# Row 0's last tiles turned on another engine, fewer warming matmuls, and a new order of issue in a residual layer kernel

## The chip, the core and the metric

The kernel runs on one core of a Trainium2 chip, in one launch. The metric is the time of one execution on the device in microseconds, lower is better. TensorE (PE) multiplies matrices; VectorE (DVE), ScalarE (ACT) and GpSimd (POOL) work elementwise; SyncE (SP) issues nearly all DMAs, from one queue. Each of these engines takes its instructions strictly in the order in which they were issued, and waits on semaphores for what others make.

## The reference

```python
def _L0_cond_ref(hidden0, hidden1, x, W, b):
    hidden = jnp.concatenate([hidden0, hidden1], axis=-1)
    x_mean = jnp.mean(x, axis=1, keepdims=True)
    ...
    fused = jnp.concatenate([x, x_mean * ones_L, hidden[:, None, :] * ones_L], axis=-1)
    relation = jax.nn.relu(jnp.einsum('bld,do->blo', fused, W) + b)
    return relation
x = x + _L0_cond_ref(cond_512, cond_512, x, L0_cond_W, L0_cond_b)
```

x is 4 rows (batch) of 1024 positions of 512 numbers, W is 1536 by 512, all in 32-bit floats. The product splits into three: x times the first third of W, at every position; the mean of x over a row's positions times the second third, once a row; and the conditioning vector (used twice, 256 numbers) times the last third, once a row. The last two, with b, are one bias vector a row. The output is x plus the relu of product and bias.

## The kernel before, in words

**Tiles.** A tile is 128 positions of one row: 8 tiles a row, 32 in all. TensorE needs x with its 512 inputs on the partitions, in four chunks j of 128, so each tile is first turned (transposed), then multiplied. For accuracy x and W are each split in a high part that TensorE takes in its fast 32-bit format and the rest, a low part, and a chunk's product is three matmuls of 128x128 by 128x512: hi by w_hi, lo by w_hi, hi by w_lo (`product`, line 544). A tile takes 12 of them into one PSUM bank; 32 tiles take 384, of which the last tile's are cut in two column halves (24 matmuls of 256 columns and the same work).

**Two ways to turn.** A unit is 1 to 4 tiles of one row that are turned together, and a piece is what one split works on. Units listed in `BY_PE` are turned by TensorE: `turn` (line 428) issues one transpose of 128x128 per tile and chunk against an identity, from the x tile that is loaded as it lies. The others are turned by VectorE (line 441) from z, the same numbers loaded a second time in another arrangement, by four DMAs a unit (four quarters of 32 partitions in runs of 512 bytes); VectorE's transpose handles one chunk of a unit at a time. Row 0 is units 0 to 3 (tiles 0 to 3, one tile each, all four chunks in a piece) and unit 4 (tiles 4 to 7, a piece per chunk); all five are in `BY_PE`. The six units of rows 1 to 3 go by VectorE. Pieces are held in PSUM (two buffers, so a piece waits until the low part of the one two before it has been made) or, of VectorE's, every second in SBUF.

**What follows.** ScalarE writes hi (`split_hi`, line 446) and, for pieces of one chunk, adds up the positions in the same instruction; VectorE or GpSimd writes lo (`split_lo`, line 465). For the four whole-tile pieces VectorE adds up (`add_up`). When a row's pieces have been added up, VectorE reduces them to the total, ScalarE scales it and starts an accumulator with the conditioning part, VectorE runs four mean steps against w_mean (line 506), and upper, fold, rows_hi and rows_lo, on ScalarE and VectorE in turn, make two 64-partition operands; TensorE's bias product (`pb`, line 526) adds over the partitions and spreads the row's bias; ScalarE copies it. Then each accumulator is emptied: the first ten tiles (`PARK`) by a plain copy on ScalarE (line 570), since the bias is late, then bias, relu and x on GpSimd and ScalarE; others by VectorE with the bias; those in `BIAS_FIRST` start from a bias written ahead into the bank and need one VectorE instruction at the end. There are five accumulator banks, so a tile's first product waits until the tile five before it is emptied.

**Weights.** W's first third comes in four loads of 256 KB, each split in w_hi (ScalarE or VectorE, lines 419 and 421) and w_lo (VectorE or GpSimd, line 424). The first eight DMAs of SP are x tile 0, W 0, W 1, x 1, W 2, W 3, x 2, x 3.

**Warming.** `fill` (line 357) is a matmul of zeros into a bank that nothing reads. Five are issued at the start, and further ones wherever a model of the time, kept by the kernel, finds TensorE idle in its first 12 us (lines 602 to 604).

**What sets the order.** `make_plan` lists some 520 tasks with the engines that each may run on, a cost for each, and what it depends on. `ORDER` is a list of numbers: twice the task's number, plus one where the second of its engines is taken. The program is issued in that order, so it fixes every engine's sequence, SP's loads and stores among them, and the costs only place the warming matmuls. `PORTION` says in how many tiles' portions an x group of four is loaded (here: group 0 tile by tile, groups 5 to 7 in halves).

Of the kernel before, what the change touches and what calls it, by code (L numbers as in the profile page):

```python
# [23 lines left out]
G = 4  # L24
# [3 lines left out]
PORTION = {0: 1, 5: 2, 6: 2, 7: 2}  # L28
# [7 lines left out]
ROW0 = [(0, k, 1) for k in range(4)] + [(0, 4, G)]  # L36
# [61 lines left out]
SP = {"sp": (0.42, 0.42)}  # L98
ZQ = {"sp": (0.42, 0.42)}
MB = 2.62  # L100
# [24 lines left out]
def make_plan():  # L125
    plan = Plan()
    after = {}
    loads = [
        (("x", 0, 0), MB / 4), (("w", 0), MB / 4 + 1.6), (("w", 1), MB / 4 + 0.5), (("w", 2), MB / 4),
# [9 lines left out]
    first = list(chain.values())  # L139
    for s in range(2):  # L140
        plan.add(("w_cond", s), SP, [], pipe=MB / 2, soft=[("w_cond", 0)] if s else first)
    plan.add(("w_mean",), SP, [], pipe=MB + 0.5, soft=first)
# [16 lines left out]
    for n, g in enumerate(x_slots):  # L159
# [8 lines left out]
        for i in range(0, G, portion(g)):  # L168
            plan.add(("x", g, i), SP, deps, pipe=MB * portion(g) / G,
                     soft=chain + ([("w_cond", 1)] if n > x_slots.index("cond") else []))  # L170
# [6 lines left out]
    for c, (u, js) in enumerate(PIECES):  # L177
        r, k0, n = UNITS[u]
        whole = len(js) > 1
        w = n * len(js)  # L180
# [132 lines left out]
def kernel(  # L313
# [286 lines left out]
    for s, e, key in log:  # L600
        if e == "pe":
            if s < WARM_TO and s - pe_free > 0.35:
                for _ in range(int((s - pe_free - 0.1) / 0.22)):
                    fill()
            pe_free = s + plan.tasks[key][0][e][0]
        emit[key[0]](e, *key[1:])
# [28 lines left out]
```

## Time and profile before

| | us |
|---|---|
| runs, median (lowest, highest) | 107.23 (106.7, 107.62) |
| the profiled execution, its time | 106.93 |
| its span from first to last instruction | 105.1 |
| TensorE busy in it | 100.9 |
| VectorE busy | 73.7 |
| GpSimd busy | 71.2 |
| ScalarE busy | 61.3 |

The profile is one execution. A row of the timeline reads: start, how long, engine, line, operation, output from input, shapes, count; in square brackets the idle time just ahead and what ended it. A row of a stretch reads: from:to, length, and then for each engine in turn (PE, PEld, DVE, ACT, POOL) its busy time and number of instructions, last the granted clock, the DMA engines' share and their rate. A row of a group has busy time and mean nanoseconds of one behind the first bar, idle time ahead of it behind the second. PE's matmuls overlap (one of 512 columns is shown as 0.40 us long), so the distance of two starts tells more than a length. PEld is the load of the stationary operand, which overlaps PE.

### The profile page before, as it was taken

The page shows a single profiled execution, that of the slowest core. Times are in us where ns is not written, and L with a number is a line of the kernel's source. Part 1 is how long each engine was busy: PE and PEld are TensorE (multiplying, and loading weights), DVE is VectorE, ACT ScalarE, POOL GpSimd, SP SyncE. Part 2 cuts the span into 40 slices and gives each one's busy share as a digit, 9 for nine tenths or more (in the row PEclk, how much of TensorE's full clock was granted, in tenths as well). Part 3 has the DMA queues.
Part 4 walks back from the last instruction along what each step waited for, and adds up shares of the span by engine and source line. Part 5 has one row for each costly group of instructions (what it writes and reads, how often), then busy time and mean ns, then how long its engine had stood idle before and what let it go on. Part 6 is the DMA issues. An engine that isn't in the chain of part 4 may idle for free.

```text
span 105.1 us, 1449 instructions
## 1 busy us (share of the span) xinstructions
PE 100.9 (96%) x448; PEld 79.6 (76%) x448; DVE 73.7 (70%) x107; ACT 61.3 (58%) x136; POOL 71.2 (68%) x64
## 2 busy tenths in 40 slices
PE   5999999999999999999999999999999999999980
PEld 2447887888788878887888788788878887888870
DVE  1086575276999968999999999999989704500450
ACT  5244426899687997789995660999602206930000
POOL 6000407949748999999999999999999800791000
PEclk9999999999999999999999999999999999999999
DMA  3799999999999999999999999927989989755442
GB/s 65 224 305 379 388 417 252 171 200 197 201 176 235 169 202 203 204 204 225 356 390 388 215 199 274 368 108 235 342 262 375 403 280 306 280 212 199 157 161 81
DMA packets 23025, 26.31 MB, mean 250 GB/s; under 512 B 1253, under 2 KB 13801, under 8 KB 22890
## 3 DMA queue, kind: packets, MB, share of 16 engines
q1 hardware_dynamic: 23010, 26.22, 94.5%
q8 instruction: 3, 0.05, 0.2%
q14 instruction: 4, 0.03, 0.1%
q10 hardware_dynamic: 8, 0.00, 0.0%
HBM read 17.83 MB, written 8.39 MB: 249 GB/s over the span
## 4 chain that ended last, share of the span: by engine, by line
PE 96%; DVE 1%; issue 0%
PE po_None L554 83%; PE pw L358 5%; PE xT L439 4%; PE po L554 3%; PE pb L526 1%; DVE o L568 0%; DVE warm L346 0%; PE pt L475 0%; DVE one L348 0%
## 5 line engine op out<-in xcount | busy, mean ns | idle before, releaser
L554 PE MATMUL po_None<-w_hi,hi 128*128 128x512 f32 x124 | 48.8, 400 | 0.0
L554 PE MATMUL po_None<-w_hi,lo 128*128 128x512 f32 x124 | 48.7, 397 | 0.0
L554 PE MATMUL po_None<-w_lo,hi 128*128 128x512 f32 x124 | 48.4, 398 | 0.0
L581 POOL TENSOR_TENSOR o<-o,x 128x512 f32<-128x512 f32 x22 | 27.9, 1309 | 6.3 <-ACT o L578 6.3
L554 PEld LDWEIGHTS po_None<-w_hi,hi 128*128 128x128 f32 x124 | 23.3, 188 | 5.8 <-DVE w_hi L421 0.3
L554 PEld LDWEIGHTS po_None<-w_lo,hi 128*128 128x128 f32 x124 | 23.3, 188 | 5.5
L554 PEld LDWEIGHTS po_None<-w_hi,lo 128*128 128x128 f32 x124 | 23.3, 188 | 5.2
L441 DVE STREAM_TRANSPOSE xT<-z 128x512 f32<-128x512 f32 x24 | 25.1, 1090 | 1.0 <-DMA z<-in_x_dram 1.0
L452 ACT ACTIVATE hi<-xT 128x512 fp32r<-128x512 f32 x32 | 19.3, 608 | 8.6 <-PE xT L439 6.7
L468 POOL TENSOR_TENSOR lo<-xT,hi 128x512 fp32r<-128x512 f32 x12 | 15.5, 1313 | 2.4 <-ACT hi L452 2.3
L468 DVE TENSOR_TENSOR lo<-xT,hi 128x512 fp32r<-128x512 f32 x20 | 13.2, 678 | 4.1 <-ACT hi L452 4.0
L578 ACT ACTIVATE o<-o 128x512 f32<-128x512 f32 x22 | 13.4, 623 | 1.0 <-DVE o L572 0.6
L506 DVE SCALAR_TENSOR_TENSOR acc<-w_mean,tot,acc 128x512 f32<-128x512 f32 x16 | 12.1, 755 | 2.5 <-ACT acc L503 1.8
L575 POOL TENSOR_TENSOR o<-o,bias 128x512 f32<-128x512 f32 x10 | 12.9, 1312 | 0.1
L572 DVE TENSOR_TENSOR o<-po_None,bias 128x512 f32<-128x512 f32 x12 | 7.8, 675 | 5.0 <-issue 5.0
L568 DVE SCALAR_TENSOR_TENSOR o<-po_None,x 128x512 f32<-128x512 f32 x9 | 5.9, 682 | 7.1 <-PE po_None L554 5.6
L530 ACT ACTIVATE bias<-pb 128x512 f32<-128x512 f32 x4 | 2.4, 600 | 9.1 <-PE pb L526 9.1
L358 PE MATMUL pw<-warm 128*128 128x512 bf16 x14 | 5.8, 569 | 1.2 <-DVE one L348 1.2
L570 ACT ACTIVATE o<-po_None 128x512 f32<-128x512 f32 x10 | 5.6, 600 | 2.1 <-PE po_None L554 2.1
L424 POOL TENSOR_TENSOR w_lo<-w_x,w_hi 128x512 fp32r<-128x512 f32 x1 | 1.3, 1296 | 8.1 <-ACT w_hi L419 8.1
L461 DVE TENSOR_REDUCE sums<-xT 128x4 f32<-128x512 f32 x4 | 2.8, 689 | 5.1 <-ACT hi L452 5.1
L487 ACT ACTIVATE term<-wc,cT 128x512 f32<-128x512 f32 x8 | 5.5, 717 | 1.0 <-POOL wc L483 1.0
(45 smaller groups left out, 74.0 us busy)
## 6 DMA issues: line engine op xcount, KB each, us to landing
out_dram<-o SPq DMA_DIRECT2D x31, 256.0 KB, 5.7
z<-in_x_dram SPq DMA_DIRECT2D x24, 256.0 KB, 11.5
x<-in_x_dram SPq DMA_DIRECT2D x4, 1024.0 KB, 9.9
x<-in_x_dram SPq DMA_DIRECT2D x6, 512.0 KB, 7.2
x<-in_x_dram SPq DMA_DIRECT2D x4, 256.0 KB, 6.8
w_x<-in_L_cond_W_dram SPq DMA_DIRECT2D x4, 256.0 KB, 5.7
w_cond<-in_L_cond_W_dram SPq DMA_DIRECT2D x2, 512.0 KB, 8.2
w_mean<-in_L_cond_W_dram SPq DMA_DIRECT2D x1, 1024.0 KB, 12.2
```

The lines of the kernel that those rows point to most:

```text
L358: nc.tensor.matmul(pw, lhsT=warm[:, :P], rhs=warm, start=True, stop=True)
L441: nc.vector.transpose(v[:, : n * P].rearrange("p (n t) -> p n t", t=Q), zs[u].rearrange("p n (a j) -> p n j a", j=J)[:, : n * NQ, js[0], :],)
L452: nc.scalar.activation(hi[c][:, :m], xT[c][:, :m], AF.Copy, accum_out=sums[:, r, js[0], s : s + 1] if len(js) == 1 else None,)
L468: eng[e].tensor_tensor(lo[c][:, :m], xT[c][:, :m], hi[c][:, :m].bitcast(F32), ALU.subtract)
L506: nc.vector.scalar_tensor_tensor(acc[r], w_mean[:, j, :], totals[r][:, j : j + 1], acc[r], ALU.mult, ALU.add)
L554: nc.tensor.matmul(v[:, : m.shape[-1]], lhsT=(hi, lo, hi)[n][p][:, c * P : (c + 1) * P], rhs=m, start=(t not in BIAS_FIRST and i == 1), st ...
L568: nc.vector.scalar_tensor_tensor(o_tile(t)[:, d], v, 0.0, x_tile(t)[:, d], ALU.max, ALU.add)
L570: nc.scalar.activation(o_tile(t), v, AF.Copy)
L572: nc.vector.tensor_tensor(o_tile(t), v, biases[t // NK], ALU.add)
L575: nc.gpsimd.tensor_tensor(outs[t], outs[t], biases[t // NK], ALU.add)
L578: nc.scalar.activation(outs[t], outs[t], AF.Relu)
L581: nc.gpsimd.tensor_tensor(outs[t], outs[t], x_tile(t), ALU.add)
```

## The change

Tiles 4 to 7 were one unit turned by TensorE. They become two units of two tiles: tiles 4 and 5 are still turned by TensorE (`BY_PE` stays 0 to 4, and unit 4 is now the half), tiles 6 and 7 are unit 5, which is turned by VectorE from z. So eight transposes leave TensorE, four stream transposes of 256 columns come to VectorE, four z loads of 128 KB to SP, and x's second group is loaded in two halves, tiles 6 and 7 much later (they are needed at the end alone); the sixth group, before in two halves, is now loaded whole. Unit 4's pieces are half as wide, unit 5 adds four more: four hi and four lo of 512 columns become eight and eight of 256. The rule for warming matmuls asks for a longer gap and puts fewer in it. The order is a new list; the costs in the load table only shift the model.

```diff
-PORTION = {0: 1, 5: 2, 6: 2, 7: 2}
+PORTION = {0:1,1:2,6:2,7:2}
...
-ROW0 = [(0, k, 1) for k in range(4)] + [(0, 4, G)]
+ROW0 = [(0,k,1) for k in range(4)]+[(0,4,2),(0,6,2)]
...
-        (("x", 0, 0), MB / 4), (("w", 0), MB / 4 + 1.6), (("w", 1), MB / 4 + 0.5), (("w", 2), MB / 4),
+        (("x", 0, 0), MB / 4 + 0.25), (("w", 0), MB / 4 + 1.2), (("w", 1), MB / 4 + 1.0), (("w", 2), MB / 4 + 0.2),
...
-    plan.add(("w_mean",), SP, [], pipe=MB + 0.5, soft=first)
+    plan.add(("w_mean",), SP, [], pipe=MB + 0.8, soft=first)
...
-0 2 4 10 16 6 8 12 110 14 74 112 18 20 116 24 94 114 22 454 26 96 456 98 28 458 30 118 100 32 460 103 34 462 120
+0 2 4 10 16 6 8 12 118 14 120 18 103 122 486 105 488 124 82 20 490 106 24 108 492 111 113 26 28 126 128 494 496
...
             if s < WARM_TO and s - pe_free > 0.35:
-                for _ in range(int((s - pe_free - 0.1) / 0.22)):
+                for _ in range(int((s - pe_free - 0.35) / 0.43)):
                     fill()
```

The new list is one line longer, so behind it every line's number is higher by one: line 554 of the products is 555 there, 439 of the transposes 440. Three of the four w_lo are now GpSimd's (before, one), and three of the four w_hi VectorE's (before, one). In SP's order, behind the first eight loads, stood x's second group, the two w_cond, b, w_mean and row 1's z; now w_cond's first half, x's tiles 4 and 5, w_cond's second half, b, the four new z, w_mean, row 1's z.

The first place is TensorE at the head, from the last warming matmul behind tile 0's transposes to tile 1's transposes. pw is the warming matmuls' bank, po_None an accumulator, xT the turned x, a number behind a name its allocation. Before:

```order
L358 MATMUL pw<-warm 128x512
L554 MATMUL po_None<-w_hi,hi_134 128x512
L554 MATMUL po_None<-w_hi,lo_135 128x512
L358 LDWEIGHTS warm
L358 MATMUL pw<-warm 128x512
L554 MATMUL po_None<-w_lo,hi_134 128x512
L439 MATMUL xT_164<-ident,x_116 128x128 x4
```

And now:

```order
L359 MATMUL pw<-warm 128x512
L555 MATMUL po_None<-w_hi,hi_132 128x512
L555 MATMUL po_None<-w_hi,lo_133 128x512
L555 MATMUL po_None<-w_lo,hi_132 128x512
L555 MATMUL po_None<-w_hi,hi_132 128x512
L440 MATMUL xT_160<-ident,x_116 128x128 x4
```

The warming matmul between the second and the third product is gone, and a fourth product has moved ahead of the transposes; ahead of the piece, eight warming matmuls have become three.

The second place is VectorE around row 0's total (tot), its mean steps (acc from w_mean) and the first turns. Before:

```order
L468 TENSOR_TENSOR lo_257<-xT_245,hi_256 128x512
L468 TENSOR_TENSOR lo_290<-xT_275,hi_289 128x512
L496 TENSOR_REDUCE tot_306<-sums 128x4
L468 TENSOR_TENSOR lo_297<-xT_284,hi_296 128x512
L506 SCALAR_TENSOR_TENSOR acc_312<-w_mean,tot_306,acc_312 128x512 x4
L441 STREAM_TRANSPOSE xT_351<-z_155 128x512
L516 TENSOR_TENSOR acc_312<-acc_312,upper_353 64x512
```

And now:

```order
L442 STREAM_TRANSPOSE xT_293<-z_157 128x256
L442 STREAM_TRANSPOSE xT_295<-z_157 128x256
L442 STREAM_TRANSPOSE xT_306<-z_157 128x256
L469 TENSOR_TENSOR lo_304<-xT_295,hi_303 128x256
L497 TENSOR_REDUCE tot_312<-sums 128x4
L469 TENSOR_TENSOR lo_298<-xT_291,hi_297 128x256
L507 SCALAR_TENSOR_TENSOR acc_315<-w_mean,tot_312,acc_315 128x512 x4
L517 TENSOR_TENSOR acc_315<-acc_315,upper_360 64x512
L523 TENSOR_TENSOR rows<-acc_315,rows 64x512
L442 STREAM_TRANSPOSE xT_398<-z_240 128x512
```

The four turns of tiles 6 and 7 (the first is one row further up) now stand ahead of the total, and row 1's first turn (z_155 before, z_240 now) has moved behind fold and rows_lo.

The third place is ScalarE over the same time: the splits of the last pieces of row 0, the accumulator copies (o from po_None) and the conditioning's weighings (term). Before:

```order
L487 ACTIVATE term_1_282<-wc,cT 128x512
L452 ACTIVATE hi_289,sums<-xT_275 128x512
L452 ACTIVATE hi_296,sums<-xT_284 128x512
L570 ACTIVATE o_303<-po_None 128x512
L499 ACTIVATE tot_306<-tot_306 128x4
L503 ACTIVATE acc_312<-cond_280 128x512
```

And now:

```order
L453 ACTIVATE hi_297,sums<-xT_291 128x256
L453 ACTIVATE hi_300,sums<-xT_293 128x256
L453 ACTIVATE hi_303,sums<-xT_295 128x256
L453 ACTIVATE hi_308,sums<-xT_306 128x256
L504 ACTIVATE acc_315<-cond_287 128x512
L500 ACTIVATE tot_312<-tot_312 128x4
L488 ACTIVATE term_1_328<-wc,cT 128x512
L571 ACTIVATE o_330<-po_None 128x512
```

The second accumulator copy of the program (o_303 before, o_330 now, tile 1's) stood ahead of the total's scaling; now it stands behind the four hi of tiles 6 and 7, the accumulator's start, the scaling and a weighing.

37 rows, old and new, of the table ORDER are left out of this document.

## The prediction

> **What bounds the kernel now.** I read the page first, for shares and for the chain of waits.
>
> ```profile
> span 105.1 us, 1449 instructions
> PE 100.9 (96%) x448; PEld 79.6 (76%) x448; DVE 73.7 (70%) x107; ACT 61.3 (58%) x136; POOL 71.2 (68%) x64
> ...
> PE 96%; DVE 1%; issue 0%
> ```
>
> TensorE carries the chain. Whether it ever stands inside its 96% is for the chain in order of time and the busy time by stretches; I cut the stretches at the first product, at a product that waits, and where the waiting seems over.
>
> ```profile
> 7.08:9.43 2.35, 2.35 (x14) 1.61 (x12) 1.19 (x4) 0.92 (x2) 0.00 (x0) 1.00 1.04 344
> 9.43:12.26 2.83, 2.83 (x17) 2.52 (x17) 1.87 (x3) 1.10 (x3) 1.30 (x1) 1.00 1.05 395
> 12.26:101.97 89.71, 89.71 (x407) 72.96 (x405) 67.93 (x95) 56.26 (x129) 68.29 (x54) 1.00 0.99 252
> ```
>
> ```profile
> 65.49 21.71 PE po_None L554 x93
> ```
>
> 93 products in 21.71 us are 0.2334 us each, and from 12.26 on TensorE has no idle time: one instruction fewer there is its whole time saved. Busy time hides short waits, since a matmul of 0.40 us overlaps the next, so for the head I read TensorE's timeline by starts. (Row 0's products and the transposes are single rows; w_hi, w_lo are the split weights, hi, lo the split x.)
>
> ```profile
> 1.19 2.32 PE L358 MATMUL pw<-warm 128*128 128x512 bf16 x5 [1.19 <-DVE one L348]
> 3.47 1.10 PE L439 MATMUL xT<-ident,x 128*128 128x128 f32 x4
> 4.37 3.06 PE L358 MATMUL pw<-warm 128*128 128x512 bf16 x8
> 7.08 0.58 PE L554 MATMUL po_None<-w_hi,hi 128*128 128x512 f32 x1
> ...
> 9.14 0.39 PE L554 MATMUL po_None<-w_lo,hi 128*128 128x512 f32 x1
> 9.43 0.50 PE L554 MATMUL po_None<-w_hi,hi 128*128 128x512 f32 x1
> ...
> 11.87 0.64 PE L439 MATMUL xT<-ident,x 128*128 128x128 f32 x4
> 12.26 0.48 PE L554 MATMUL po_None<-w_hi,hi 128*128 128x512 f32 x1
> ...
> 18.63 1.12 PE L439 MATMUL xT<-ident,x 128*128 128x128 f32 x8
> 19.51 0.48 PE L554 MATMUL po_None<-w_lo,hi 128*128 128x512 f32 x1
> 19.82 0.40 PE L554 MATMUL po_None<-w_hi,lo 128*128 128x512 f32 x1
> ...
> 101.85 0.28 PE L554 MATMUL po<-w_lo,hi 128*128 128x256 f32 x1
> ```
>
> Two things: the warming matmuls stand before the first product and end just as it starts; and the seventh product, at 9.43, is the first one that a load decides. VectorE's timeline says which:
>
> ```profile
> 8.94 0.43 DVE L421 CAST w_hi<-w_x 128x512 fp32r<-128x512 f32 x1 [0.78 <-DMA w_x<-in_L_cond_W_dram]
> ```
>
> The third quarter of W lands at 8.94, its w_hi is made by 9.37, and TensorE goes on at 9.43.
>
> **The change part by part.**
>
> *Eight transposes fewer, the term that pays.* Tiles 4 to 7 cost TensorE 16 transposes, in two groups of 8. From 18.63 to 19.51 is 0.88; the product behind it takes 0.31 to the next start instead of 0.233, 0.08 more: 0.96 a group, 0.12 each. Now VectorE turns tiles 6 and 7, eight transposes go: **-0.97**, on the stretch without idle time.
>
> *Fewer warming matmuls, worth nothing in this execution.* By the orders on TensorE shown with the change, three warming matmuls stand behind the first transposes instead of eight, none between products, and a fourth product comes ahead of tile 1's transposes. What then decides each product:
>
> ```profile
> 4.61 0.60 ACT L452 ACTIVATE hi<-xT 128x512 fp32r<-128x512 f32 x1 [2.38 <-PE xT L439]
> 5.32 0.63 ACT L419 ACTIVATE w_hi<-w_x 128x512 fp32r<-128x512 f32 x1
> 6.81 0.63 ACT L419 ACTIVATE w_hi<-w_x 128x512 fp32r<-128x512 f32 x1 [0.86 <-DMA w_x<-in_L_cond_W_dram]
> ...
> 10.35 1.30 POOL L424 TENSOR_TENSOR w_lo<-w_x,w_hi 128x512 fp32r<-128x512 f32 x1 [8.08 <-ACT w_hi L419]
> ```
>
> The eight first loads keep their order. W's first quarter is there by 5.32; w_hi now comes by VectorE's cast (0.43): product 1 at 5.8, lo (0.68) product 2 at 6.4, w_lo by GpSimd (1.30) product 3 at 7.2, the second w_hi at 7.44 product 4 at 7.5, tile 1's transposes to 8.1, products 5 and 6 by 8.6. Product 7 waits for the same cast at 8.94: 9.43, as before. Behind it stand as many products and transposes as before up to 12.26 (14 and 16). So 1.3 us of earlier start ends in a wait of 0.9 us: **0**. GpSimd's other two w_lo, at 9.4 and 10.7, end by 12.0; TensorE asks for them at 13.0 and 14.4.
>
> The price in speed: five first warming matmuls in 2.32 us are (2.32 - 0.63) / 4 = 0.42 apart, double 0.2334 for as wide an operand. Eight in the 2.71 us from 4.37 to 7.08 fit 0.42 and then 0.22 with the turn near 6.5, though the granted-clock column reads 1.00 throughout. In the forecast this half speed costs nothing: even at 0.42, products 1 to 6 and four transposes end by 9.3, ahead of the load.
> [...]
>
> *What VectorE, ScalarE and the queue take on.* By VectorE's order, four half-width turns stand ahead of row 0's total and its mean chain, and the turns of row 1 now come behind that whole chain. Prices and landings:
>
> ```profile
> L441 DVE STREAM_TRANSPOSE xT<-z 128x512 f32<-128x512 f32 x24 | 25.1, 1090 | 1.0 <-DMA z<-in_x_dram 1.0
> L468 DVE TENSOR_TENSOR lo<-xT,hi 128x512 fp32r<-128x512 f32 x20 | 13.2, 678 | 4.1 <-ACT hi L452 4.0
> L506 DVE SCALAR_TENSOR_TENSOR acc<-w_mean,tot,acc 128x512 f32<-128x512 f32 x16 | 12.1, 755 | 2.5 <-ACT acc L503 1.8
> L542 ACT ACTIVATE po<-bias 128x256 f32<-128x256 f32 x2 | 0.7, 366 | 0.0
> ```
>
> ```profile
> 16.50 2.55 POOL L483 TENSOR_TENSOR wc<-w_cond 128x512 f32<-128x512 f32 x2 [4.86 <-DMA w_cond<-in_L_cond_W_dram]
> ```
>
> ```profile
> 20.42 0.69 DVE L468 TENSOR_TENSOR lo<-xT,hi 128x512 fp32r<-128x512 f32 x1 [2.27 <-ACT hi L452]
> ...
> 22.37 3.13 DVE L506 SCALAR_TENSOR_TENSOR acc<-w_mean,tot,acc 128x512 f32<-128x512 f32 x4 [0.56 <-ACT acc L503]
> 26.45 1.11 DVE L441 STREAM_TRANSPOSE xT<-z 128x512 f32<-128x512 f32 x1 [0.96 <-DMA z<-in_x_dram]
> ```
>
> ```profile
> L412 SPq DMA_DIRECT2D w_mean<-in_L_cond_W_dram x1: 357/357/357, 8.9 to 8.9; - x1
> ...
> DMA to landing us min/median/max: 12.2/12.2/12.2
> ```
>
> ```profile
> L386 SPq DMA_DIRECT2D x<-in_x_dram x1: 383/383/383, 5.3 to 5.3; - x1
> ...
> DMA to landing us min/median/max: 8.4/8.4/8.4
> ```
>
> A turn of 256 columns costs between 0.55 (half of 1.09) and 1.09; I take 0.55, since a copy of 128x256 takes 0.37 beside 0.60 whole. Four are 2.2 us, in a stretch where VectorE idled 2.27 and 0.96.
> When do the new z quarters land? w_mean landed at 8.9 + 12.2 = 21.1, row 1's four z by 26.45: 1.33 per 256 KB. w_cond landed at 16.5; x's second group, ahead of it, at 5.3 + 8.4 = 13.7, so w_cond's megabyte took 2.75. Half of that x no longer stands ahead, about 1.35 less: 15.1. Half a megabyte of z: 17.8. The upper bound: w_mean needed 4.6 where a megabyte takes 2.75, so a landing can lag 2: 19.8.
> At 17.8: turns to 20.0, the last hi near 21.4, total and scaling 22.1, four mean steps (3.13) 25.3, then upper, fold, rows_hi, rows_lo (0.6 to 0.7 each, on two engines, with other work of ScalarE's between) 28.5. TensorE comes to the bias product after 67 products from 12.26, the eight remaining transposes and the conditioning pair: 12.26 + 15.6 + 1.4 = 29.3. Spare: 0.8. Row 1's z land near 27.8 (1.33 later, for half a megabyte of z in place of half of x); VectorE turns from 28.4, the first lo is ready at 32.4 behind three turns, TensorE asks at 33.2. Spare: 0.8.
> ScalarE is tightest, since it is strictly in order. Tile 1's accumulator copy (o_330) stands behind the four new hi, the accumulator start, the scaling and a weighing; tile 6's first product needs that bank (the fifth after tile 1) at 12.26 + 46 products + 1.4 = 24.4. With z at 17.8 the copy ends near 23.4, spare 1.0; at 19.8 it ends near 24.5 and the bias product's inputs near 30, a wait of 0.1 to 0.7. I take **+0.1** (0 to 0.7), nearer the early bound, because in this place w_cond precedes z and not the late w_mean.
> The tail keeps its order: the last tile's two halves, one last store. **0.** Later rows keep their instructions; SP has four more issues, and z's bytes grow by 0.5 MB, in queues that TensorE never waited for.
>
> *Sum:* -0.97 + 0 + 0.1 = -0.87 against this execution's 106.93 (span 105.1 and 1.8 around it): 106.06. The runs' median is 107.23 (106.7 to 107.62), which would give 106.36. I centre on the middle of both, **106.2**.
>
> **The rivals.**
>
> *A. The new chain through ScalarE eats the gain.* Place: o_330 behind the z turns, and the bias product. If z lands beyond 19.8, every microsecond more is one on TensorE. For it: a spare of 1.0 against a lag of up to 2 that w_mean showed. Against: nothing lagged ahead of w_mean. Landing 0.7 beyond the bound: 106.2 + 0.7 = **106.9**.
>
> *B. The speed rises late, and the change is slower.* In the trace half speed ended 5.3 us after 1.19, without a break. If a break starts the count again, the changed kernel, whose unbroken activity ends at 5.65, counts from 9.43: half speed until 14.7, 5.3 / 0.42 = 12.6 products where 22.7 fit, 10.1 x 0.233 = 2.4 us lost: 106.2 + 2.4 = **108.6**. It erases the gain from the point where more than 0.87 / 0.19 = 4.6 products run slowly after 9.43, so if the rise is later than 11.4. Against: at half speed TensorE is busy nearly all of 5.8 to 9.3 anyway.
>
> *C. The third quarter of W lands earlier in most executions.* Then the earlier start is worth something: product 7 could follow at 8.6, 0.8 sooner, **105.4**. For it: landings of W took 4.1 to 6.5 us here:
>
> ```profile
> DMA to landing us min/median/max: 4.1/5.7/6.5
> ```
>
> Against: that order of loads is untouched, and one trace shows 8.94.
>
> **How the numbers follow.** Forecast 0.6, A 0.18, B 0.11, C 0.11. One per cent, 1.07 us, is about what a measurement tells here. The forecast's 106.2 is just under it from 107.23: of its 0.6, 0.29 fall over 1%. Faster 0.29 + 0.11 = 0.40; same 0.31 + 0.18 = 0.49; slower 0.11. The range, 105.4 to 107.3, takes in C, A, and the spread of the runs shown, and leaves B out.
>
> **What would show it.** Right: 24 transposes at 0.12 each, product 7 again at about 9.4 behind VectorE's cast, 12.26 unchanged, no idle TensorE behind it, the last product near 101.0 instead of 101.85, the bias product near 29.3. Wrong: a wait of tile 6's first product or the bias product (A), starts 0.42 apart behind 9.43 (B), product 7 before 9 (C), or a wait of row 1's first lo.

## The result: 0.6% faster, and the profile after

| | before | after |
|---|---|---|
| runs, median (lowest, highest), us | 107.06 (106.09, 108.76), 12 runs | 106.38 (105.52, 108.27), 12 runs |
| the profiled execution, its time | 106.93 | 106.00 |
| its span | 105.1 | 104.2 |
| TensorE busy in it | 100.9 | 99.3 |
| last product starts | 101.85 | 100.66 |

The ratio of the times is 0.9936, 95% interval [0.9908, 0.9965]: 0.68 us less, between 0.37 and 0.98. All ratios below are to the kernel before, run beside on the same chip, and leave out executions that took over 1.5% more than the fastest of the same kernel, which are 3 of the 12 of the changed kernel here and 0 to 9 of a kernel's executions below. The kernels were timed on several chips; the text says where two of them shared one.

The page of the changed kernel, in the lines that answer to those of before:

```profile
span 104.2 us, 1439 instructions
PE 99.3 (95%) x434; PEld 77.9 (75%) x434; DVE 75.3 (72%) x113; ACT 60.9 (58%) x142; POOL 75.0 (72%) x68
...
PE 90%; DMA 4%; POOL 1%; DVE 1%; SPq 0%; issue 0%
```

TensorE still carries the chain, with 14 instructions fewer (eight transposes and six warming matmuls), but 4% of the chain is now a load, W's, where the first products used to stand behind warming matmuls. The same three stretches, cut at product 1, product 7 and the first product behind tile 3's transposes (product 15):

```profile
6.17:9.12 2.95, 2.78 (x10) 1.76 (x11) 2.17 (x4) 0.90 (x2) 1.24 (x2) 1.00 1.00 382
9.12:11.92 2.80, 2.80 (x17) 2.42 (x17) 2.05 (x4) 0.93 (x2) 2.44 (x2) 1.00 1.05 394
11.92:100.78 88.86, 88.86 (x399) 71.98 (x397) 69.67 (x101) 56.99 (x136) 69.64 (x57) 1.00 1.01 261
```

The middle stretch is as long as before (2.80 against 2.83), the last one 0.85 shorter: it begins 0.34 earlier and the last product starts 1.19 earlier. TensorE's timeline of the changed kernel, by starts:

```profile
4.45 1.48 PE L359 MATMUL pw<-warm 128*128 128x512 bf16 x3
6.17 0.77 PE L555 MATMUL po_None<-w_hi,hi 128*128 128x512 f32 x1 [0.24 <-DVE w_hi L422]
...
8.89 0.40 PE L555 MATMUL po_None<-w_lo,hi 128*128 128x512 f32 x1
9.12 0.46 PE L555 MATMUL po_None<-w_hi,hi 128*128 128x512 f32 x1
...
13.41 0.39 PE L555 MATMUL po_None<-w_hi,hi 128*128 128x512 f32 x1
13.73 0.48 PE L440 MATMUL xT<-ident,x 128*128 128x128 f32 x2
...
28.90 0.40 PE L555 MATMUL po_None<-w_lo,hi 128*128 128x512 f32 x1
29.14 0.40 PE L527 MATMUL pb<-rows,ones 128*128 128x512 f32 x1
...
100.66 0.28 PE L555 MATMUL po<-w_lo,hi 128*128 128x256 f32 x1
```

Product 1 is 0.91 earlier and product 7 is 0.31 earlier. Tile 4's transposes start 0.32 behind the product ahead of them instead of 0.23: a wait of 0.09 for their x, which was not there before. The bias product (29.14) follows without a gap. VectorE's timeline shows what set the head and what the new chain cost:

```profile
5.60 0.43 DVE L422 CAST w_hi<-w_x 128x512 fp32r<-128x512 f32 x1 [4.32 <-DMA w_x<-in_L_cond_W_dram]
...
8.59 0.43 DVE L422 CAST w_hi<-w_x 128x512 fp32r<-128x512 f32 x1
...
19.29 2.21 DVE L442 STREAM_TRANSPOSE xT<-z 128x256 f32<-128x256 f32 x4
...
22.86 3.13 DVE L507 SCALAR_TENSOR_TENSOR acc<-w_mean,tot,acc 128x512 f32<-128x512 f32 x4 [0.27 <-DMA w_mean<-in_L_cond_W_dram]
```

The cast of W's third quarter starts at 8.59 (8.94 before), since the load landed earlier in this execution; product 7 follows it. The four turns are 0.55 us each. The mean steps wait for w_mean.

One part of the time lies behind the last transfer. These are SP's last events by the trace (start in us, the semaphores waited for), with the landing of the last store; no view of the page lists them:

```
before: 104.31 last store landed (semaphore 110)
        103.00 106 | 103.06 107, 105 | 103.12 108, 104 | 103.23 109, 101 | 104.33 110, 100 | 105.15 end
after:  103.13 last store landed (semaphore 106)
        103.14 106 | 103.20 107, 105 | 103.27 108, 104 | 103.33 109, 101 | 103.39 110, 100 | 104.22 end
```

In both traces SP checks the DMAs' semaphores at the end in the same order, some 0.065 us a step where none is waited for (the times are those at which a step was through). Before, the last store had the one that is checked last, and the other checks were over by then. The changed kernel has four transfers more (84 in its trace, 80 before), which moves the last store on to the one that is checked first, so four checks follow its landing: from landing to end it is 1.09 us instead of 0.84.

So the profiled pair's -0.93 is, to 0.01, -0.34 (head), -0.85 (behind product 15) and +0.25 (end).

### The profile page after: what moved, and what is told of

It reads as the page before. It is cut to its first block, busy times and chain, and to the rows that moved or that the text cites. A ratio compares the mean times of both kernels' runs of the same rounds, so it can differ in the third digit from the quotient of the medians.

```text
span 104.2 us, 1439 instructions
## 1 busy us (share of the span) xinstructions
PE 99.3 (95%) x434; PEld 77.9 (75%) x434; DVE 75.3 (72%) x113; ACT 60.9 (58%) x142; POOL 75.0 (72%) x68
## 4 chain that ended last, share of the span: by engine, by line
PE 90%; DMA 4%; POOL 1%; DVE 1%; SPq 0%; issue 0%
PE po_None L555 83%; DMA w_x<-in_L_cond_W_dram 4%; PE po L555 3%; PE xT L440 2%; POOL w_lo L425 1%; PE pb L527 1%; DVE w_hi L422 0%; DVE o L569 0%; SPq L387 0%; PE pt L476 0%
## 5 line engine op out<-in xcount | busy, mean ns | idle before, releaser
L555 PE MATMUL po_None<-w_hi,hi 128*128 128x512 f32 x124 | 49.4, 402 | 0.2 <-DVE w_hi L422 0.2
L555 PE MATMUL po_None<-w_hi,lo 128*128 128x512 f32 x124 | 49.3, 399 | 0.0
L442 DVE STREAM_TRANSPOSE xT<-z 128x512 f32<-128x512 f32 (+1 forms) x28 | 27.5, 1027 | 0.1
L453 ACT ACTIVATE hi<-xT 128x512 fp32r<-128x512 f32 (+1 forms) x36 | 20.0, 559 | 10.0 <-PE xT L440 7.1
L469 POOL TENSOR_TENSOR lo<-xT,hi 128x512 fp32r<-128x512 f32 (+1 forms) x14 | 17.0, 1218 | 0.8 <-ACT hi L453 0.8
L469 DVE TENSOR_TENSOR lo<-xT,hi 128x512 fp32r<-128x512 f32 (+1 forms) x22 | 13.1, 601 | 3.3 <-ACT hi L453 3.2
L425 POOL TENSOR_TENSOR w_lo<-w_x,w_hi 128x512 fp32r<-128x512 f32 x3 | 3.9, 1285 | 5.9 <-DVE w_hi L422 5.9
L513 ACT ACTIVATE upper<-acc 64x512 f32<-64x512 f32 x4 | 2.4, 598 | 7.3 <-DVE acc L507 7.2
L453 ACT ACTIVATION_READ_ACCUMULATOR hi<-xT 128x1 f32 x32 | 6.2, 192 | 0.0
```

The costliest lines, as they stand in the source:

```text
L442: nc.vector.transpose(v[:, : n * P].rearrange("p (n t) -> p n t", t=Q), zs[u].rearrange("p n (a j) -> p n j a", j=J)[:, : n * NQ, js[0], :],)
L453: nc.scalar.activation(hi[c][:, :m], xT[c][:, :m], AF.Copy, accum_out=sums[:, r, js[0], s : s + 1] if len(js) == 1 else None,)
L469: eng[e].tensor_tensor(lo[c][:, :m], xT[c][:, :m], hi[c][:, :m].bitcast(F32), ALU.subtract)
L555: nc.tensor.matmul(v[:, : m.shape[-1]], lhsT=(hi, lo, hi)[n][p][:, c * P : (c + 1) * P], rhs=m, start=(t not in BIAS_FIRST and i == 1), st ...
```

## The experiments

All but the second start from the changed kernel; the edit of each is shown.

**The old rule for warming matmuls.**

```diff
-                for _ in range(int((s - pe_free - 0.35) / 0.43)):
+                for _ in range(int((s - pe_free - 0.1) / 0.22)):
```

> The changed kernel with the old rule for warming matmuls (15 in all instead of 8; 7 instead of 3 behind tile 0's transposes, 3 more between the first products). Theory (the head waits for W's third quarter, the warming matmuls are cover): the first product moves from 6.2 to about 7.0, product 7 from 9.1 to between 9.1 and 9.5, since products 1 to 6 now end just after the load instead of before it; time +0.0 to +0.4 us on the changed kernel. Rival (the earlier start is what pays): the 0.9 us come back, ratio to the kernel before near 1.00.

Measured: 0.9934 [0.99, 0.9968]. TensorE's timeline of this kernel:

```profile
9.64 0.39 PE L555 MATMUL po_None<-w_hi,hi 128*128 128x512 f32 x1
...
12.41 0.48 PE L555 MATMUL po_None<-w_hi,hi 128*128 128x512 f32 x1
...
101.03 0.28 PE L555 MATMUL po<-w_lo,hi 128*128 128x256 f32 x1
```

Product 7 is 0.5 later than in the changed kernel's trace, though W's third quarter was cast earlier (by 8.83, there by 9.02): in this execution it stood behind the matmuls ahead of it and not behind the load. The ratio is the same, but it rests on seven of twelve executions, and the median of all twelve, 106.73, is only 0.2% under the 106.95 of the kernel before; the two rules are alike within some 0.4%. From product 15 to the last product it is 88.62, against 89.59 before: 0.97 less, with no wait in between.

**The new rule alone**, in the kernel before.

```diff
-                for _ in range(int((s - pe_free - 0.1) / 0.22)):
+                for _ in range(int((s - pe_free - 0.35) / 0.43)):
```

> The kernel before with only the new rule for warming matmuls (8 instead of 14). Theory: first product from 7.08 to about 6.0, product 7 stays at the landing of W's third quarter plus 0.5 us (near 9.4), all behind it as before; ratio to the kernel before 1.000 (0.998 to 1.002). Rival (earlier start pays): 0.991. Rival (half speed lasts longer without them): 1.01 to 1.02, with starts 0.42 apart behind 9.4.

Measured: 0.9984 [0.9951, 1.0017]. TensorE's timeline:

```profile
6.08 0.79 PE L554 MATMUL po_None<-w_hi,hi 128*128 128x512 f32 x1 [0.25 <-ACT w_hi L419]
...
9.00 0.39 PE L554 MATMUL po_None<-w_hi,hi 128*128 128x512 f32 x1
...
11.73 0.48 PE L554 MATMUL po_None<-w_hi,hi 128*128 128x512 f32 x1
...
101.30 0.28 PE L554 MATMUL po<-w_lo,hi 128*128 128x256 f32 x1
```

From 11.73 to 101.30 are 89.57, as before. The rule is worth nothing that these times can tell, with either order; the gain is the order's.

**Tiles 4 and 5 transposed twice on TensorE**, the second time into the same place: the eight transposes are back, and nothing else is.

```diff
-                    nc.tensor.transpose(v[:, (m * n + i) * P : (m * n + i + 1) * P], x_t[:, j], ident)
+                    for _ in range(2 if u == 4 else 1):
+                        nc.tensor.transpose(v[:, (m * n + i) * P : (m * n + i + 1) * P], x_t[:, j], ident)
```

> The changed kernel with the eight transposes of tiles 4 and 5 issued twice, into the same place, so that TensorE has 32 transposes again and nothing else changes. Theory: 8 x 0.12 = +0.97 us on the changed kernel, of which up to 0.1 may lie in TensorE's short wait for x's tiles 4 and 5; ratio to the kernel before near 1.002. Rival (the gain came from the order or the warming): the changed kernel's time, ratio near 0.994.

Measured: 1.0015 [0.9981, 1.0048], 0.79% above the changed kernel, some 0.85 us, which by the two intervals together is known to some 0.5 us. TensorE's timeline:

```profile
12.19 0.48 PE L556 MATMUL po_None<-w_hi,hi 128*128 128x512 f32 x1
...
13.68 0.39 PE L556 MATMUL po_None<-w_hi,hi 128*128 128x512 f32 x1
14.50 0.72 PE L441 MATMUL xT<-ident,x 128*128 128x128 f32 x4 [0.43 <-DVE sums L463]
...
102.42 0.28 PE L556 MATMUL po<-w_lo,hi 128*128 128x256 f32 x1
```

From 12.19 to 102.42 are 90.23, of which 0.59 is the wait ahead of tile 4's transposes (0.82 between starts less 0.23; by the trace's DMA events their x landed at 14.36, so the releaser named is not the one). The 89.64 left are 1.02 above the 88.62 of the kernel without waits. The eight transposes carry the gain.

**The last store back on the semaphore that is checked last**, by loading four x groups in halves (four transfers more, the same data).

```diff
-        nc.sync.dma_start(out=xs[g][:, i : i + n], in_=xv[r, :, k + i : k + i + n, :])
+        for a in range(i, i + n, 2 if n == G else n):
+            d = slice(a, a + (2 if n == G else n))
+            nc.sync.dma_start(out=xs[g][:, d], in_=xv[r, :, k + d.start : k + d.stop, :])
```

> The changed kernel with the four x groups that are loaded whole (2 to 5) loaded in two halves each, four DMAs more, so that the last store gets again the last of the eight semaphores that SP checks in turn at the end. Theory (the end costs 0.26 us more because the last store's semaphore is checked first and the others after it): last landing to the span's end falls from 1.05 to about 0.79 us, ratio to the kernel before near 0.991. Rival (the end's difference is chance, or a DMA's): stays at 1.05, ratio 0.994.

Measured: landing at 104.38, end at 105.21: 0.83 us between them, as the theory has it. The time does not settle more: the ratio of 0.9898 [0.984, 0.9957] rests on three of twelve executions (105.36, 105.63, 106.62), the others took 107.0 to 109.0.

**The changed kernel again**, for the spread.

> The changed kernel itself once more, beside the next three on one chip. Theory (transposes pay 0.85 to 0.97, the end gives 0.26 back): ratio to the kernel before 0.991 to 0.996, and a wider spread of its executions than of the kernel before's, since it waits for two landings (W's third quarter, x's tiles 4 and 5) where the kernel before waits for one. Rival (the spread of the first runs was chance): the same spread as the kernel before.

Measured: 0.9928 [0.989, 0.9966], median 106.24. The spread is wider, as expected: the twelve executions have a standard deviation of 0.7 us, the 35 of the kernel before beside them 0.5. Its trace, TensorE's timeline, has a wait that the first one had not:

```profile
28.93 0.40 PE L555 MATMUL po_None<-w_lo,hi 128*128 128x512 f32 x1
29.61 0.47 PE L527 MATMUL pb<-rows,ones 128*128 128x512 f32 x1 [0.28 <-DVE rows L523]
```

0.68 between starts is 0.45 of idle time ahead of the bias product.

**x of tiles 4 and 5 loaded ahead of w_cond** (82 is that load in the order's list, 18 is w_cond's first half).

```diff
-0 2 4 10 16 6 8 12 118 14 120 18 103 122 486 105 488 124 82 20 490 106
+0 2 4 10 16 6 8 12 118 14 120 82 18 103 122 486 105 488 124 20 490 106
```

> The changed kernel with the load of x's tiles 4 and 5 moved ahead of w_cond's first half in SP's order, nothing else. Theory (TensorE's wait ahead of tile 4's transposes is for this load, which the new order put 1.3 us later): the load lands near 12.3, the wait (0.1 in the first trace, 0.6 in another) is gone, w_cond as a whole lands as before; time -0.1 to -0.4 us on the changed kernel and a narrower spread. Rival (that wait is for the PSUM buffer, not the load): unchanged.

Measured: 0.9928 [0.9886, 0.997], on the chip of the run before: no difference. TensorE's timeline:

```profile
13.60 0.40 PE L560 MATMUL po_None<-w_hi,hi 128*128 128x512 f32 x1
13.84 0.39 PE L445 MATMUL xT<-ident,x 128*128 128x128 f32 x2
...
29.24 0.39 PE L560 MATMUL po_None<-w_lo,hi 128*128 128x512 f32 x1
30.22 0.47 PE L532 MATMUL pb<-rows,ones 128*128 128x512 f32 x1 [0.59 <-DVE rows L528]
```

The load landed at 12.16, and the wait at tile 4's transposes is gone (0.24 between starts), but the bias product waits 0.75.

**No warming at all.**

```diff
-S_BUFS, O_BANKS, Z_BUFS, X_BUFS, O_BUFS, N_WARM = 14, 5, 3, 5, 13, 5
+S_BUFS, O_BANKS, Z_BUFS, X_BUFS, O_BUFS, N_WARM = 14, 5, 3, 5, 13, 0
...
-WARM_TO = 12.0
+WARM_TO = 0.0
```

> The changed kernel without any warming matmul. Theory of windows (some 3.4 us of near-unbroken activity lift the half speed): TensorE is busy from about 5.9 on at half speed, so matmul starts 0.42 apart until between 9.3 and 12.7, and the time is 0 to 1.6 us above the changed kernel. Rival theory (5.3 us without a break are needed, each break starts the count again): half speed to 14 or later, 2 us or more. Rival (warming is worth nothing): same time.

Measured: 1.0035 [1.0004, 1.0067], on the same chip as the two above, 1.08% over the changed kernel. The matmuls that the change kept do earn their place. TensorE's timeline:

```profile
5.91 0.77 PE L555 MATMUL po_None<-w_hi,hi 128*128 128x512 f32 x1 [1.20 <-DVE w_hi L422]
6.47 0.74 PE L555 MATMUL po_None<-w_hi,lo 128*128 128x512 f32 x1
...
9.40 0.39 PE L555 MATMUL po_None<-w_lo,hi 128*128 128x512 f32 x1
9.63 0.40 PE L555 MATMUL po_None<-w_hi,hi 128*128 128x512 f32 x1
```

The first two products are 0.56 apart, and at 9.40 the step is 0.23. The trace's record of the clock has full speed from 9.29, 3.38 us behind the start of the first product, so in this trace the first theory holds, and neither rival does. Where the 1% lies this trace does not show: its product 7 stands 0.62 behind the landing of W's third quarter (9.01), in the changed kernel's trace 0.55.

**Warming matmuls between the first products**, where the first loads are waited for.

```diff
-    pe_free = 99.0
+    pe_free, n_products = 99.0, 0
...
+        n_products += key[0] == "product"
+        if key[0] == "product" and n_products in (1, 2, 3, 6):
+            fill()
```

> The changed kernel with four more warming matmuls, one behind each of the products 1, 2, 3 and 6 in row 0's first tiles, where TensorE waits. Theory (executions of the changed kernel with a mean granted clock of 0.984 are those where TensorE's waits in the head bring half speed back for one stretch of about 3.4 us, worth 1.7 us): no execution at 0.984, the rest of the executions as the changed kernel's, +0 to +0.2 us. Rival (0.984 is the chip's doing): still one execution in ten at 0.984.

Measured: 0.9926 [0.9891, 0.9961], median 106.07, same chip: not to be told from the changed kernel. None of its executions had a mean granted clock of 0.984. The bias product waited 0.56 in its trace.

**One product moved ahead of the bias product** (380 is the bias product, 602 tile 6's third).

```diff
-380 198 602 382
+198 602 380 382
```

> The changed kernel with one product (tile 6, third piece, 0.70 us) moved ahead of row 0's bias product on TensorE, nothing else. Theory: the bias product waits for w_mean, about 6.1 us after that load lands (landed 22.75, 23.52, 23.88 in three traces; bias product at 29.14 without a wait, 29.61, 29.96), and TensorE stands until then; with a product of 0.70 us put into the wait, no idle time over 0.1 us is left ahead of the bias product where the load lands by 23.8, and the time falls by 0 to 0.6 us, most likely 0.3: ratio 0.990 to before, where the changed kernel had 0.993 to 0.994. Rival: the time lost at the bias product is made up later anyway, since the row sums on the other engines set the pace; then the last product ends as before and the ratio stays at 0.993.

Measured: 0.9949 [0.9918, 0.9981]: the gain that was expected is not there, and the rival's 0.993 lies inside. TensorE's timeline:

```profile
30.67 0.40 PE L560 MATMUL po_None<-w_lo,hi 128*128 128x512 f32 x1
30.90 0.40 PE L532 MATMUL pb<-rows,ones 128*128 128x512 f32 x1
...
64.06 0.40 PE L560 MATMUL po_None<-w_lo,hi 128*128 128x512 f32 x1
64.58 0.49 PE L560 MATMUL po_None<-w_hi,hi 128*128 128x512 f32 x1
```

The place is filled (0.23 between starts), so that half of the theory holds. The trace has 0.62 of idle time ahead of it, at tile 4's transposes (0.85 between starts), and 0.29 far behind.

**w_mean loaded one transfer later** (22 is w_mean, 34 the next quarter of z).

```diff
-22 150 540 508 152 532 550 156 836 154 530 158 342 346 558 34
+150 540 508 152 532 550 156 836 154 530 158 342 346 558 34 22
```

> The changed kernel with the load of w_mean issued one load later, behind the first quarter of the z of tiles 8 to 11 (1.3 us of the queues). Theory: the landing of w_mean sets row 0's bias product, and it has no spare left: w_mean lands at 24.0 to 25.2, the bias product starts 6.1 us later, at 30.2 to 31.3, after 1.0 to 2.2 us without work on TensorE, and the last product ends later by as much: about +1.3 us against the changed kernel, ratio 1.005. Rival, the step of the prediction: the bias product has 0.8 us of spare, so that only 0.5 us is lost: ratio 0.998. Third: w_mean isn't what it waits for; then nothing changes, 0.993.

Measured: 0.99 [0.9844, 0.9955] in four executions. Of the three expectations only the last lies inside the interval, and the trace says why the first failed: VectorE's mean steps began earlier than in the changed kernel's trace, not later.

```profile
22.53 3.13 DVE L512 SCALAR_TENSOR_TENSOR acc<-w_mean,tot,acc 128x512 f32<-128x512 f32 x4
```

By the trace's DMA events the sixteen parts of w_mean landed from 20.37 to 21.70; in the changed kernel's trace, from 19.54 to 22.75. The first part came 0.83 later and the last 1.05 earlier, so the mean steps began with the total's scaling (22.50) and not with w_mean. What delayed the load in the changed kernel's trace is the last of its parts, not its place in the queue. This was the only trace with so narrow a spread (1.3 us where the others with the changed order have 3.0 to 4.6), so a single execution cannot tell whether the move makes it narrow, and the price of this place stays open. The same trace has a late head, on TensorE:

```profile
4.63 1.06 PE L364 MATMUL pw<-warm 128*128 128x512 bf16 x2
6.37 0.77 PE L560 MATMUL po_None<-w_hi,hi 128*128 128x512 f32 x1 [0.67 <-DVE w_hi L427]
6.93 0.74 PE L560 MATMUL po_None<-w_hi,lo 128*128 128x512 f32 x1
7.63 0.80 PE L560 MATMUL po_None<-w_lo,hi 128*128 128x512 f32 x1
8.23 0.63 PE L560 MATMUL po_None<-w_hi,hi 128*128 128x512 f32 x1
...
9.36 0.74 PE L560 MATMUL po_None<-w_hi,lo 128*128 128x512 f32 x1
9.94 0.39 PE L560 MATMUL po_None<-w_lo,hi 128*128 128x512 f32 x1
10.16 0.39 PE L560 MATMUL po_None<-w_hi,hi 128*128 128x512 f32 x1
...
29.98 0.39 PE L532 MATMUL pb<-rows,ones 128*128 128x512 f32 x1
...
101.53 0.28 PE L560 MATMUL po<-w_lo,hi 128*128 128x256 f32 x1
```

Product 2 stands behind VectorE's low part and product 3 behind GpSimd's w_lo (7.58); the steps that waited for nothing are 0.60 (product 4) and 0.58 (product 6) until 9.94, and 0.22 from there. Half speed lasted 3 us longer than in the changed kernel's trace (the clock's record has full speed from 9.93, there from 6.89), and product 7 came at 10.16, though W's third quarter had been cast by 8.46 (its load landed at 7.81).

**Three edits together**: x first, warming between products, one product ahead of the bias product (the three diffs above).

> The changed kernel with three edits: the x of tiles 4 and 5 loaded ahead of w_cond, warming matmuls also behind products 1, 2, 3 and 6, and one product ahead of row 0's bias product. Theory: the wait at tile 4's transposes (0.1 to 0.3 us) goes, the bias product's wait (0 to 0.75 us) is filled but for 0.1, and no execution has a half-speed window: median about 105.8, ratio 0.989, no execution at a mean clock of 0.984. Rival: the edits move the waits to the product that follows (tile 6's first, which waits for VectorE), and the ratio stays at 0.993.

Measured: 0.9952 [0.9919, 0.9985]. TensorE's timeline:

```profile
24.16 0.40 PE L560 MATMUL po_None<-w_lo,hi 128*128 128x512 f32 x1
24.71 0.50 PE L560 MATMUL po_None<-w_hi,hi 128*128 128x512 f32 x1 [0.16 <-ACT o L576]
...
33.68 0.40 PE L560 MATMUL po_None<-w_hi,hi 128*128 128x512 f32 x1
34.26 0.50 PE L560 MATMUL po_None<-w_hi,lo 128*128 128x512 f32 x1 [0.18 <-DVE lo L474]
```

The rival expectation holds, except that the wait at tile 6's first product is for ScalarE and not for VectorE. Of the waits that the edits were to remove, 0.17 is left at the bias product, but 0.32 stand at tile 6's first product, behind ScalarE's accumulator copy, and 0.35 at row 1's first low part, which VectorE makes.

**The three edits and the last store's semaphore** (the same, and four x groups in halves).

> As the kernel with three edits, and four groups of x each loaded by two transfers, so that the last store's semaphore is the last that SP checks at the end. Theory: end less last landing 0.83 us where it was 1.09, and nothing else moves: 0.26 us less than the kernel with three edits, ratio 0.987. Rival: what is saved at the end is lost to the four more transfers, whose issues take 0.43 us each on SP ahead of other loads: the same ratio as the three edits alone, or a little more.

Measured: 0.9947 [0.9907, 0.9986]. Landing at 104.52, end at 105.36: 0.84 again. The median is 105.91 where the three edits alone, on the same chip, have 106.22. The difference of 0.31 has the size of the 0.25, but is less than the spread of either (standard deviations of 0.5 and 0.7), so the time alone does not show it. No version was measurably faster than the changed kernel.

## Why the prediction was right, step by step

**Eight transposes fewer, -0.97: right.** From product 15 to the last product it is 0.97 less in the kernel with the old warming rule, which has no wait there, and 0.85 less in the changed kernel, of which 0.09 is the new wait at tile 4. With the eight put back it is 1.02 more, and 0.79% of the time.

**Fewer warming matmuls, 0: right in the sum, with too small a price behind it.** With either order, the two kernels that differ in the rule alone cannot be told apart. The reason given holds in the changed kernel's trace: product 1 moved to 6.17 and product 7 still stood behind the third quarter of W. What the prediction said beside it, that even at 0.42 a product the first six end by 9.3, ahead of the load, did not hold everywhere. In the trace with the late head W's first quarter let product 1 start at 6.37, not 5.8; products at half speed that waited for nothing were 0.58 to 0.60 apart, not 0.42, which was the distance of warming matmuls; and product 7 came at 10.16, 1.0 us later than in the changed kernel's trace, with its load long there.

**VectorE, ScalarE and the queue, +0.1 (0 to 0.7): the size held, the gate was another.** z landed at 19.04, inside 17.8 to 19.8, and a turn took 0.55. The working had the mean steps begin at 22.1, behind the total, with a spare of 0.8 for the bias product. They began at 22.86, because w_mean, which stands behind the four new z, landed at 22.75. The total was scaled by 22.65, on ScalarE:

```profile
22.46 0.19 ACT L500 ACTIVATE tot<-tot 128x4 f32<-128x4 f32 x1
```

So w_mean cost 0.2 here; in the three traces of the table in which the bias product waited, the total was scaled 0.6 to 0.9 ahead of the start. From the start of the mean steps to a bias product that was waited for it is 5.97 or 5.98 us in all six traces that have such a wait (the three others are the kernels without warming, with three edits, and with these and the last store's semaphore), so in the changed kernel's trace it was ready at 28.84 and the spare was 0.3:

| trace | mean steps start | bias product | idle ahead of it |
|---|---|---|---|
| w_mean one transfer later | 22.53 | 29.98 | 0 |
| the old warming rule | 22.76 | 29.48 | 0 |
| the changed kernel | 22.86 | 29.14 | 0 |
| the changed kernel again | 23.63 | 29.61 | 0.45 |
| warming between products | 23.99 | 29.96 | 0.56 |
| x ahead of w_cond | 24.24 | 30.22 | 0.75 |

That is the bias product's wait, the second place of rival A, and its 0.45 to 0.75 is about the 0.1 to 0.7 that the working gave for a late z (19.5 to 19.9 in these three traces), but for another reason: the working had z decide, not w_mean. A's first place, tile 6's first product, shows in the kernel with three edits, and so does a wait of row 1's first low part, which the prediction had among its signs of being wrong. What these waits cost in the median is not shown: edits that filled them did not move it measurably. From the changed kernel's second timing on, every profiled execution was slower than its kernel's median, by 0.3 to 1.3 us, so these waits are those of slower executions. One wait was missed: tile 4's x landed at 13.59 in the changed kernel's trace (12.6 to 14.8 in the others with this order of loads), TensorE came to it at 13.64, and over the traces it waited 0 to 0.6 us there. Before, that load landed at 13.67 and was wanted only at 15.4.

**The tail, 0: wrong.** "The tail keeps its order" is true of the stores, but the number of DMAs in the program decides on which semaphore the last one falls. It gave back 0.25 in the trace; that the times follow is not shown.

**The sum.** Predicted was -0.87 against the profiled execution. The changed kernel's profiled execution shows -0.93, made otherwise: -0.34 in the head, where a quarter of W landed 0.35 sooner, -0.94 from the transposes, +0.09 at tile 4 and +0.25 at the end. The first of these needed an early landing, which is no part of the change (it ranged from 7.8 to 9.4 over the traces), and the earlier start as well: before, product 6 started at 9.14, so product 7 could have come no sooner than 9.37 (a product is 0.23), and with the old rule it came at 9.64 behind a load cast by 8.83. That is rival C in a small size; product 7 never came before 9.0, and the times do not show it. Without it -0.60 is left, and the measured ratio says -0.68. That -0.93 came so near to -0.87 is luck: an early landing and a longer end, neither in the sum, nearly cancel. Against the ratio the forecast was some 0.2 us too hopeful, which is inside that measurement's interval (0.37 to 0.98); the tail's 0.25 is the missed term of that size.

**Rival B, a late rise of the speed, is real, but was seen in one execution and is smaller than priced.** By the trace's record of the clock, full speed began at 6.73 in the kernel before, at 6.89 in the changed kernel and at 9.93 in the trace with the late head. At full speed the records have 98.987 us on end in the first two of these, and 95.573 in a trace of the experiments: 3.414 less, and the lengths are 29.0 and 28.0 times that difference. TensorE was busy for 0.92 to 1.00 of the 3.41 us ahead of the rise in every trace. In the one with the late head, W's first quarter landed 0.2 later than in the changed kernel's trace, TensorE stood idle from 5.69 to 6.37, the 3.41 us from 3.10 to 6.52 were 0.80 busy, and the rise came 3.41 us behind them, at 9.93. With the old rule, warming matmuls would stand in that gap; this was not tried on such a landing. Product 7 came 1.0 us later, where B had 2.4 lost. How much activity is enough, and from when it counts, no run shows: B's 5.3 us without a break was the author's estimate from the trace of before, and without warming the rise came 3.38 us behind the first product.

## What to carry to other kernels

Where one engine has no idle time, instructions taken off it are worth their whole start-to-start distance, here 0.12 us for a transpose, and the forecast's risk lies in the waits that the new order opens. For each of these compare the time at which an operand is asked for with the last landing of several traces, not of one, and ask it of each load in the chain, w_mean here as well as z. Count the DMAs too: the last store's place among the semaphores is part of the end, here 1.09 us behind its landing against 0.84.

## What the runs showed of the hardware

- SP's checks of the eight DMA semaphores at the end came in the same order before and after the change, a step every 0.065 us or so where none was waited for. From the last landing to the end it is 1.08 to 1.09 us where the last store has the one checked first, and 0.83 to 0.84 where it has the one checked last, in every trace of this study.
- The sixteen parts of w_mean's megabyte landed within 1.3 us of each other in one execution and within 3.0 to 4.6 in the others with the new order. The same quarter of W landed between 7.8 and 9.4 us.
- Nine of 76 executions with the new order and the new warming rule as it is have a mean granted clock of 0.984 or less; one stretch of 3.41 us at half speed in the span would make 0.984 (1 - 3.41 / 2 / 106), an estimate with the difference of the two recorded lengths above. They took 107.35 to 109.03 us. None of 99 of the kernel before do, none of 12 of it with the new rule, none of 10 without any warming, and none of 48 with the new order and more warming (the old rule, or matmuls between products). That more warming prevents it is likely but not shown: 40 of the executions ran on a chip on which none had it, whatever the rule, and on the two others that timed both it is 8 of 48 against 0 of 24. No such execution was profiled, so when such a stretch falls is not known. The mean does not count the head: the execution with the late head has 1.0.
